# A state-space mixer beside a ternary FFN: segment sums moved into the FFN stage, steps 0 to 10 and the end put in another order

## The chip, the cores and the metric

The kernel runs on one NeuronCore of a Trainium2 chip. The core has a matrix engine (PE, with its weight loads listed as PEld), a vector engine (DVE), a scalar engine for activations and copies (ACT), a general engine (POOL) and a sync engine (SP). SP's work here is to issue DMAs; POOL issues some too. Each engine works through its own queue in order, and semaphores tie the queues together. The metric is the device time of one execution in microseconds (us); lower is better.

## The reference

The input is `x` of 4 batches of 256 tokens with 512 features. A layer norm gives `xn`; the result is `x + s * silu(f)`. `f` is a gated FFN of inner width 1792 with ternary weights, and `s` is a Mamba-2 mixer with 128 heads of 64, 8 groups and a state of 128:

```
zxbcdt = xn @ in_proj_w.T                       # gate 8192 | x 8192, B 1024, C 1024 | dt 128
xBC    = silu(conv1d(xBC, 4 taps) + conv_b)     # x, B, C
dt     = softplus(dt + dt_bias);  Adt = -exp(A_log) * dt
L      = exp(segment_sum(Adt))                  # out[i, j] = sum of Adt over m = j+1 .. i
y      = (C B^T * L) @ (x * dt) + carried state + D * x
y      = y * silu(gate); y = y * rsqrt(mean(y^2 over a group) + eps) * norm_w
s      = y @ out_proj_w.T
f      = (silu(xn @ gate_w.T) * (xn @ up_w.T)) @ down_w.T
```

The segment sum is what the change is about. It makes, for each head, a lower triangle of partial sums along 128 positions out of one row of `Adt`, and its exponential is the decay mask.

## The kernel before, in words

All of it is float32, tokens along the free dimension: `xnT` holds the normalised input transposed, 128 features by 1024 tokens, four times. The projection is cut into tiles of 128 output features. One tile of x is two heads, so there are 64 tiles (`CT`), 8 to a group (`PER_G`). A tile's gate and x features are projected together by a scheme of seven products instead of eight (`product`, L170); it needs four sums of weight blocks per tile (`combine_to`, L139 to L147, called s1, s2, s4, s3).

There are two stages. The first, `front` (L189 to L573), normalises x and runs the FFN. It has 28 FFN steps (14 tiles of the inner width, twice over half of the tokens); each has three places where `next(pieces)` (L540, L551, L564) puts in one **turn** of side work. `all_pieces` (L481) deals this side work out: dt and its rows (`dt_pieces`), then eight chains `bc_pieces`, one per group, that start every eight turns from turn 11 on, project B and C, convolve them and store the masked scores `C B^T`. A chain is 14 turns long, so two overlap. From turn 20 on `early_pieces` (L469) works beside them: it loads the weights of tiles 1 to 11, forms the four weight sums on DVE (tiles `wq` and `sq`) and stores them in the DRAM tile `early`. FFN weights come as int32 on SP's queue, two FFN steps ahead (`load_ffn`), and POOL casts them (`cast_ffn`, L225).

The second stage is the main loop (L766): 64 **steps**, one per tile, and two more that drain it. Step i projects tile i, makes the segment sums of tile i (`decay_scan`, L612), finishes tile i-1 (transposes, `values_0`, `values_1`, the mask `meet`, the products `y_products`, L655) and gates tile i-2 (`y_gate`, L668). From step 10 on it also carries the output projection of a group that is complete (`project_out`, two steps for each batch, eight steps for a group). The row of a head is loaded to all partitions (`load_rows`, L595), scanned on DVE, exponentiated on ACT (`decay_exp`) and multiplied with the scores (`gm`). `LEAD` (9) tells until which tile SiLU and the exponentials wait for the next step; `EARLY` (11) until which tile the stored weight sums are read.

The order on each engine is the program's order (`tc.manual_schedule`); what a step issues first on an engine stands first in that engine's queue. Tiles come from pools with few buffers, and a tile waits for the last reader of the one whose buffer it takes: the rows `m` have five, projection weights `w` two, PSUM banks `ps_proj` three, `ps_o` two, `ps_y` two, `ps_t` one.

After the loop the last group is projected (L950 to L990): per batch, seven products, summed on DVE into the rows fetched from `acc`, times the FFN's result, plus x.

Of the kernel before, what the change touches and what calls it, by code (L numbers as in the profile page):

```python
# [50 lines left out]
P = 128  # L51
# [23 lines left out]
LEAD = 9  # L75
# [6 lines left out]
def mixer_ffn(ctx: ExitStack, tc: tile.TileContext, x, in_w, conv_w, conv_b, dt_bias, a_log, d_col,  # L82
# [44 lines left out]
    early = dram.tile([EARLY, P, 4, KT // 2, P], F32, name="early")  # L127
# [59 lines left out]


    def front(pre, one_of, fp, f2, hp, wq):  # L189
# [279 lines left out]
        def early_pieces():  # L469
            for n in range(EARLY):  # L470
                w = wq.tile([P, 2, KT, P], F32, name="wq")
                for m, i in enumerate((n + 1, CT + n + 1)):
                    nc.sync.dma_start(w[:, m], in_w[i])
                for _ in range(2):
                    yield
                s = wq.tile([P, 4, KT // 2, P], F32, name="sq")
                yield from combine_to(s[:, 0], s[:, 1], s[:, 2], s[:, 3], w)
                nc.sync.dma_start(early[n], s)
                yield

        def all_pieces():  # L481
# [3 lines left out]
            while chains or later or turn < 11 + 8 * G:  # L485
# [4 lines left out]
                if turn == 20:  # L490
                    later.append(early_pieces())
# [42 lines left out]
        for n, (h, f) in enumerate(steps):  # L534
# [33 lines left out]
            last = pfs, f, hh, hl, wd  # L568
        down(*last)
# [3 lines left out]
        return held["a"]  # L573

    with (tc.manual_schedule(), tc.tile_pool(name="pre", bufs=NT) as pre,
          tc.tile_pool(name="one_of", bufs=1) as one_of, tc.tile_pool(name="fp", bufs=3) as fp,
          tc.tile_pool(name="f2", bufs=2) as f2, tc.tile_pool(name="hp", bufs=1) as hp,
          tc.tile_pool(name="wq", bufs=1) as wq):
        a = front(pre, one_of, fp, f2, hp, wq)
# [15 lines left out]
    def load_rows(ct):  # L595
        ms = []
        for h in range(2):
            m = mp.tile([P, T], F32, name="m")
            nc.sync.dma_start(m, rows[2 * ct + h, 0:T].partition_broadcast(P))
            ms.append(m)  # L600
        return ms
# [8 lines left out]

    def decay_scan(m):
        nc.vector.tensor_tensor_scan(m, m, after, 0.0, ALU.add, ALU.mult)  # L612
# [42 lines left out]
    def y_products(ps, vs, ms, offs):  # L655
# [4 lines left out]
        for b in range(NB):  # L660
            py = ps[b // 2][:, b % 2, :]
            for q, v, stop in ((0, v0, True), (1, v1, False), (1, v0t, True)):
                for h, d in enumerate(halves):
                    m = off[h][:, b, :] if v is v0t else diag[h][:, b, q, :]
                    nc.tensor.matmul(py[d, q * P:(q + 1) * P], v[:, b, h, :], m,  # L665
                                     start=False, stop=stop, skip_group_check=True)
# [9 lines left out]
    def come(k):  # L676

        return max(k // 2, k - 2)

    def norm_sums(sqacc):  # L680
        pv = ps_o.tile([P, NT], F32, name="pv", tag="o")
# [79 lines left out]
    with tc.manual_schedule():  # L761
# [3 lines left out]
        sqacc = rs = ya = outs = left = nxt = ob = sa = sb = sc = None  # L765
        for i in range(CT + 2):  # L766
            r, g = i % PER_G, i // PER_G
            here, old, older = i < CT, 0 <= i - 1 < CT, 0 <= i - 2 < CT
# [29 lines left out]
            if not here:  # L798
                project_out(lambda: None)
            if i + 1 <= EARLY:  # L800
                w = wp.tile([P, 2, KT, P], F32, name="w")
                nc.sync.dma_start(w[:, 0], in_w[i + 1])
                nc.sync.dma_start(w[:, 1, 0:2], early[i, :, 3])
                nc.sync.dma_start(w[:, 1, 2:4], in_w[CT + i + 1, :, 2:4])
            elif i + 1 < CT:
# [23 lines left out]
            if here:  # L829
# [5 lines left out]
                if i:  # L835
# [3 lines left out]
            if old:  # L839
# [5 lines left out]
                yps[i - 1] = y_begin(i - 1, xTs[i - 1])  # L845
            if here:
                product(px, s3, t3, False)
                product(pz, a12, x21, False, (1,))
                nc.scalar.copy(xpad_h[1], by_batch(px))
            if og >= 0 and on == 0:  # L850
                sd = norm_sums(sqacc)
            for k in range(PER_G):
                if wg >= 0 and wn == come(k) + 1:
                    wo = wos[wg][:, k, :]
                    nc.scalar.mul(wo, wo, nw[:, wg * PER_G + k:wg * PER_G + k + 1])
            if older:
                yf = yg.rearrange("p b l -> p (b l)")
                if (i - 2) % PER_G == 0:
                    sqacc = sqp.tile([P, T], F32, name="sqacc")
# [178 lines left out]
```

## Time and profile before

| | |
|---|---|
| median of three runs | 1774.26 us (1771.61 to 1774.85) |
| the profiled execution | 1773.71 us |
| its span, first to last instruction | 1771.7 us |
| FFN stage | to about 311 us; step 0's first product is at 308.60 |
| steps 2 to 8 | 17.27 us each (first product to first product) |
| step 9, step 10 | 18.40 and 28.66 us |
| steps 11 to 63 | 21.13 and 22.86 us in turn, 24.56 at a group's first |
| behind step 63 | from 1687.09 us |

The span is measured from the first to the last instruction of the program. In a timeline each line has the start in us, the length in us, the engine, the line of the kernel, the operation, the tiles (out <- in) and the count; in brackets stands how long the engine was idle before and what ended that. In the chain of waits, a line is a piece of the work that ended last: start, length, engine and line. In the windows the length is followed by the busy time and instruction count of PE, PEld, DVE, ACT and POOL, the granted clock of PE as a share of full speed, the DMA engines' busy share and GB/s.

### The profile page before, as it was taken

The page shows a single profiled execution, that of the slowest core. Times are in us where ns is not written, and L with a number is a line of the kernel's source. Part 1 is how long each engine was busy: PE and PEld are TensorE (multiplying, and loading weights), DVE is VectorE, ACT ScalarE, POOL GpSimd, SP SyncE. Part 2 cuts the span into 40 slices and gives each one's busy share as a digit, 9 for nine tenths or more (in the row PEclk, how much of TensorE's full clock was granted, in tenths as well). Part 3 has the DMA queues.
Part 4 walks back from the last instruction along what each step waited for, and adds up shares of the span by engine and source line. Part 5 has one row for each costly group of instructions (what it writes and reads, how often), then busy time and mean ns, then how long its engine had stood idle before and what let it go on. Part 6 is the DMA issues. An engine that isn't in the chain of part 4 may idle for free.

```text
span 1771.7 us, 22592 instructions
## 1 busy us (share of the span) xinstructions
PE 1733.2 (98%) x8494; PEld 1110.2 (63%) x8494; DVE 1447.3 (82%) x1740; ACT 1065.8 (60%) x1417; POOL 198.2 (11%) x239
## 2 busy tenths in 40 slices
PE   9999999999999999999999999999999999999989
PEld 6566666454466666666666666666666666666667
DVE  5757675799988898889888988898889888988956
ACT  4544333577666666666666666666666666666630
POOL 3221221000000000111011101110111011101110
PEclk9999999999999999999999999999999999999989
DMA  6254553567746675777676767776777677767684
GB/s 226 78 190 154 202 179 119 204 195 237 232 163 205 199 211 187 205 200 211 187 205 199 211 187 205 199 211 187 205 199 211 188 205 199 206 193 205 181 214 142
DMA packets 164235, 342.69 MB, mean 193 GB/s; under 512 B 15392, under 2 KB 55968, under 8 KB 164128
## 3 DMA queue, kind: packets, MB, share of 16 engines
q1 hardware_dynamic: 141296, 287.78, 47.0%
q0 software_dynamic: 22832, 53.49, 17.0%
q8 instruction: 67, 1.10, 0.3%
q14 instruction: 40, 0.33, 0.1%
HBM read 236.08 MB, written 76.28 MB: 176 GB/s over the span
## 4 chain that ended last, share of the span: by engine, by line
PE 85%; DVE 11%; ACT 2%; issue 2%; DMA 1%; ACTq 0%; DVEq 0%; SPq 0%
PE px L173 24%; PE po L721 22%; PE pq L173 13%; PE py L665 9%; PE pz L173 6%; PE pp L285 4%; PE tp L624 3%; DVE m L612 2%; PE pf L293 2%; DVE xT L181 2%; PE pg L460 1%; DVE cT L181 1%; PE pv L683 1%; DVE m L618 1%; DVE mo L619 1%
## 5 line engine op out<-in xcount | busy, mean ns | idle before, releaser
L612 DVE TENSOR_TENSOR_SCAN m<-m,after 128x1024 f32<-128x1024 f32 x128 | 291.9, 2281 | 0.0
L173 PE MATMUL px<-xc,w 128*128 128x512 f32 x576 | 279.2, 607 | 4.9 <-ACT xpad L424 2.7
L181 DVE SCALAR_TENSOR_TENSOR xT<-xpad,cw,xT 128x1024 f32<-128x1024 f32 x192 | 246.1, 1282 | 4.6
L721 PE MATMUL po<-wo,ya 128*128 128x256 f32 x768 | 178.4, 382 | 0.0
L173 PEld LDWEIGHTS px<-xc,w 128*128 128x128 f32 x576 | 99.3, 190 | 115.4 <-issue 69.4
L665 PE MATMUL py<-m,v 128*64 128x128 f32 x2048 | 161.9, 278 | 4.1 <-DVE v L641 4.1
L618 DVE TENSOR_TENSOR m<-m,gm 128x1024 f32<-128x1024 f32 x128 | 154.7, 1209 | 8.7 <-ACT m L615 8.7
L721 PEld LDWEIGHTS po<-wo,ya 128*128 128x128 f32 x768 | 142.6, 192 | 17.6 <-issue 0.3
L907 POOL DMA_DIRECT2D sqacc<-sq x55 | 46.9, 853 | 906.6 <-ACT sq L863 903.2
L173 PE MATMUL pz<-xnT,w 128*128 128x512 f32 x288 | 145.8, 592 | 0.0
L173 PE MATMUL px<-xc,s 128*128 128x512 f32 x288 | 137.5, 600 | 5.0 <-ACT pz L822 2.2
L173 PE MATMUL px<-xnT,w 128*128 128x512 f32 x288 | 142.0, 615 | 0.2 <-DMA w<-in_in_w 0.2
L173 PE MATMUL pq<-xnT,s 128*128 128x512 f32 x288 | 136.2, 595 | 3.3 <-DVE xpad L872 3.3
L615 ACT ACTIVATE m<-m 128x1024 f32<-128x1024 f32 x128 | 135.4, 1058 | 0.7
L173 PE MATMUL pq<-xc,s 128*128 128x512 f32 x288 | 135.4, 592 | 0.0
L665 PEld LDWEIGHTS py<-m,v 128*64 128x64 f32 x2048 | 117.8, 137 | 26.2 <-issue 19.6
L721 PE MATMUL po<-tw,sy 128*128 128x256 f32 x512 | 116.8, 381 | 0.8 <-ACT sa L775 0.8
L624 PEld LDWEIGHTS tp<-ident,xT 128*128 128x128 f32 x512 | 63.8, 141 | 71.9 <-issue 57.6
L721 PEld LDWEIGHTS po<-tw,sy 128*128 128x128 f32 x512 | 97.9, 191 | 14.7 <-ACT sa L775 1.2
L672 DVE TENSOR_TENSOR yg<-py,gT 128x512 f32<-128x512 f32 x128 | 83.8, 677 | 22.4 <-PE py L665 22.4
L832 ACT COPY gT<-px 128x512 f32<-128x512 f32 x64 | 37.4, 584 | 105.1 <-PE px L173 105.1
L173 PEld LDWEIGHTS px<-xc,s 128*128 128x128 f32 x288 | 54.7, 192 | 73.1 <-issue 65.8
(172 smaller groups left out, 3065.1 us busy)
## 6 DMA issues: line engine op xcount, KB each, us to landing
m<-rows SPq DMA_DIRECT2D x128, 512.0 KB, 6.5
w<-in_in_w SPq DMA_DIRECT2D x133, 256.0 KB, 6.8
mo<-rows SPq DMA_DIRECT2D x128, 256.0 KB, 7.2
gated<-yg SPq DMA_DIRECT2D x64, 512.0 KB, 8.2
ya<-gated SPq DMA_DIRECT2D x30, 1024.0 KB, 7.1
sqacc<-sq POOLq DMA_DIRECT2D x55, 512.0 KB, 5.7
wo<-in_out_w SPq DMA_DIRECT2D x64, 256.0 KB, 7.2
acc<-sa POOLq DMA_DIRECT2D x24, 512.0 KB, 6.0
```

The source lines that it names most:

```text
L173: nc.tensor.matmul(pp, a[:, k, :], b[:, k, :], start=start and k == 0, stop=k == KT // 2 - 1, skip_group_check=not start)
L181: nc.vector.scalar_tensor_tensor(xT, xpad[:, :, k:k + L], cw[:, i, k:k + 1], xT, ALU.mult, ALU.add)
L285: nc.tensor.matmul(pp, w[:, k * P:(k + 1) * P], part[:, k, :], start=(k == 0 and part is xh), stop=(k == KT - 1 and part is xl))
L612: nc.vector.tensor_tensor_scan(m, m, after, 0.0, ALU.add, ALU.mult)
L615: nc.scalar.activation(m, m, AF.Exp)
L618: nc.vector.tensor_mul(m, m, gm[:, 0:T])
L624: nc.tensor.transpose(tp[:, b, :], xT[:, b, c * P:(c + 1) * P], ident)
L665: nc.tensor.matmul(py[d, q * P:(q + 1) * P], v[:, b, h, :], m, start=False, stop=stop, skip_group_check=True)
L672: nc.vector.tensor_mul(yg[:, 2 * i:2 * i + 2, :], ps[i], by_batch(gT[:, i * HALF:(i + 1) * HALF]))
L721: nc.tensor.matmul(po, a[:, k, :], b[:, k, :], start=start and k == 0, stop=k == HG - 1, skip_group_check=not start)
L832: nc.scalar.copy(gT[:, HALF:], px)
L907: nc.gpsimd.dma_start(sqacc, sq, accum_op=ALU.add)
```

## The change

It has four parts.

1. **Segment sums beside the FFN.** `early` no longer holds weight sums but finished segment sums: 22 rows (two heads for each of tiles 0 to 10). `early_pieces` loads a row to all partitions (three buffers in the pool `ep`, where `wq` had one of each of two tiles), scans it in turns 2, 3 and 5 of every eight, counted from a chain's start, and stores 512 KB. The first two loads are issued in turn 18. The weight sums of the first tiles go back to the steps.
2. **Steps 0 to 10.** The main loop loads the scanned rows of these tiles and doesn't scan. In steps 0 to 9 (`fill`) the square of the gated tile goes ahead of the copy of xpad's second half, `y_begin` behind it; the weight sums for the next tile come in two halves, around the taps; the first tap goes ahead of `values_1`; and `y_products` takes the products that need v1 last. `LEAD` is 10.
3. **Tile 1's weights** are loaded at the end of the FFN, so step 0 loads none.
4. **The end.** The two draining steps are written out by hand. Tile 63's transpose goes ahead of group 6's last output products, which are dealt around it; `sa` and `sb` take buffers of `w` and `s`; the last tile is gated and squared in halves; the norm sums take the `ps_t` bank; the output weights of the last group are loaded two per step, in its first four steps.

```diff
-LEAD = 9
+LEAD = 10
...
-    early = dram.tile([EARLY, P, 4, KT // 2, P], F32, name="early")
+    early = dram.tile([2 * EARLY, P, T], F32, name="early")
...
-        def early_pieces():
-            for n in range(EARLY):
-                w = wq.tile([P, 2, KT, P], F32, name="wq")
-                for m, i in enumerate((n + 1, CT + n + 1)):
-                    nc.sync.dma_start(w[:, m], in_w[i])
-                for _ in range(2):
-                    yield
-                s = wq.tile([P, 4, KT // 2, P], F32, name="sq")
-                yield from combine_to(s[:, 0], s[:, 1], s[:, 2], s[:, 3], w)
-                nc.sync.dma_start(early[n], s)
+        def early_pieces(phases=(2, 3, 5)):
+            ms, n, turn = {}, 0, 18 - 11
+            while n < 2 * EARLY:
+                if turn % 8 in phases and turn > 9:
+                    m = ms.pop(n)
+                    decay_scan(m)
+                    nc.sync.dma_start(early[n], m)
+                    n += 1
+                for k in range(n, min(n + 2, 2 * EARLY)):
+                    if k not in ms and (turn % 8 not in phases or k == n):
+                        ms[k] = ep.tile([P, T], F32, name="em")
+                        nc.sync.dma_start(ms[k], rows[k, 0:T].partition_broadcast(P))
+                turn += 1
                 yield
...
-                if turn == 20:
+                if turn == 18:
                     later.append(early_pieces())
...
+        w = load_w(1, CT + 1)
         down(*last)
         ffn_out(1, pfs)
...
-            nc.sync.dma_start(m, rows[2 * ct + h, 0:T].partition_broadcast(P))
+            n = 2 * ct + h
+            nc.sync.dma_start(m, early[n] if ct < EARLY else rows[n, 0:T].partition_broadcast(P))
...
-    def y_products(ps, vs, ms, offs):
+    def y_products(ps, vs, ms, offs, last_v1):
...
+        parts = [(0, v0), (1, v1), (1, v0t)]
+        order = [(b, *p) for b in range(NB) for p in parts]
+        if last_v1:
+            order = [(b, *parts[n]) for ns in ((0, 2), (1,)) for b in range(NB) for n in ns]
...
-    def come(k):
-        return max(k // 2, k - 2)
+    def come(g, k):
+        return k // 2 if g == G - 1 else max(k // 2, k - 2)
...
-        for i in range(CT + 2):
+        for i in range(CT):
...
-            if i + 1 <= EARLY:
-                w = wp.tile([P, 2, KT, P], F32, name="w")
-                nc.sync.dma_start(w[:, 0], in_w[i + 1])
-                nc.sync.dma_start(w[:, 1, 0:2], early[i, :, 3])
-                nc.sync.dma_start(w[:, 1, 2:4], in_w[CT + i + 1, :, 2:4])
-            elif i + 1 < CT:
+            fill = og < 0
+            if 0 < i < CT - 1:
                 w = load_w(i + 1, CT + i + 1)
...
-                if i:
+                if i >= EARLY:
                     decay_scan(ms[i][0])
...
-                yps[i - 1] = y_begin(i - 1, xTs[i - 1])
+                if not fill:
+                    yps[i - 1] = y_begin(i - 1, xTs[i - 1])
...
+            if older and fill:
+                square()
             if here:
                 product(px, s3, t3, False)
                 product(pz, a12, x21, False, (1,))
                 nc.scalar.copy(xpad_h[1], by_batch(px))
+            if old and fill:
+                yps[i - 1] = y_begin(i - 1, xTs[i - 1])
...
-                if i == 0:
-                    decay_scan(ms[i][0])
-                    decay_scan(ms[i][1])
                 product(pq, s4, x22, False)
-            if old and og < 0:
-                vs.append(values_1(i - 1, xTs[i - 1]))
+            if fill:
+                s = scp.tile([P, 3, KT // 2, P], F32, name="s")
+                sums = combine_to(s[:, 0], s[:, 1], s[:, 2], blocks(w)[2], w)
+                a = factors(w, s)
+                next(sums)
+                xTs[i] = xtp.tile([P, NB, L], F32, name="xT")
+                last_tap(i, xTs[i], xpad)
+                conv_taps(i, xTs[i], xpad, (0,))
+                if old:
+                    vs.append(values_1(i - 1, xTs[i - 1]))
...
-                conv_taps(i, xTs[i], xpad)
+                conv_taps(i, xTs[i], xpad, (1, 2) if fill else (0, 1, 2))
...
-                if i + 1 <= EARLY:
-                    s = scp.tile([P, 3, KT // 2, P], F32, name="s")
-                    nc.sync.dma_start(s, early[i, :, 0:3])
-                    a = factors(w, s)
+                if fill:
+                    next(sums)
...
-                if i:
+                if i >= EARLY:
                     decay_scan(ms[i][1])
...
-        whole = {0: fetch(0), 1: fetch(1)}
-        yas[2] = load_gated(G - 1, 2)
+        last, ob = CT - 1, NB - 1
+        yg = y_gate(yps.pop(last - 1), gTs.pop(last - 1))
+        nc.sync.dma_start(gated[last - 1], yg.rearrange("p b l -> p (b l)"))
+        yas = {b: load_gated(G - 1, b, PER_G - 1) for b in range(2)}
+        decay_exp(ms[last][1])
+        py = y_begin(last, xTs[last])
+        vs = values_0(last, transposed(xTs[last], 0))
+        for m, off in zip(ms[last], offs[last]):
+            meet(m, off)
+        sa = wp.tile([P, NC, KT, P], F32, name="w").rearrange("p n k m -> p n (k m)")
+        sb = scp.tile([P, 3, KT // 2, P], F32, name="s")[:, 0:2].rearrange("p n k m -> p n (k m)")
+        sc = osp.tile([P, HH], F32, name="sc", bufs=2)
+        outs = out_first(left, rights[G - 2], leave)
+        for _ in range(2):
+            next(outs)
+        vs.append(values_1(last, xTs[last]))
+        sq = sqp.tile([P, T], F32, name="sq")
+        nc.scalar.activation(sq, yg.rearrange("p b l -> p (b l)"), AF.Square)
+        nc.vector.tensor_add(sqacc, sqacc, sq)
+        for _ in range(2):
+            next(outs)
+        y_products(py, vs, ms.pop(last), offs.pop(last), False)
+        rights[G - 1], toms = right_factors(wos[G - 1])
+        for make in toms[0:2]:
+            make()
+        whole = {0: fetch(0)}
+        yg, gT = ygp.tile([P, NB, L], F32, name="yg"), gTs.pop(last)
+        sq = sqp.tile([P, T], F32, name="sq")
+        for n in range(2):
+            two, to = slice(2 * n, 2 * n + 2), slice(n * HALF, (n + 1) * HALF)
+            nc.vector.tensor_mul(yg[:, two, :], py[n], by_batch(gT[:, to]))
+            nc.scalar.activation(sq[:, to], yg[:, two, :].rearrange("p b l -> p (b l)"), AF.Square)
+        nc.sync.dma_start(gated[last], yg.rearrange("p b l -> p (b l)"))
+        for n in range(2):
+            to = slice(n * HALF, (n + 1) * HALF)
+            nc.vector.tensor_add(sqacc[:, to], sqacc[:, to], sq[:, to])
         for b in range(2):
             nc.vector.tensor_copy(yas[b][:, PER_G - 1, :], yg[:, b, :])
-        sd = norm_sums(sqacc)
         left, sums = left_factors(yas[0])
-        rights[G - 1], toms = right_factors(wos[G - 1])
-        for make in (sums[0], toms[0], sums[1], toms[1], *sums[2:], *toms[2:]):
+        for make in (sums[0], sums[1], toms[2], sums[2], sums[3]):
             make()
+        for _ in outs:
+            pass
+        toms[3]()
+        rows_b = batch_rows(acc, ob)
+        nc.gpsimd.dma_start(rows_b, sa, accum_op=ALU.add)
+        nc.gpsimd.dma_start(rows_b[:, 0, :], sb.rearrange("p n c -> p (n c)"), accum_op=ALU.add)
+        nc.gpsimd.dma_start(rows_b[:, 1, HH:], sc, accum_op=ALU.add)
+        whole[1] = fetch(1)
+        yas[2] = load_gated(G - 1, 2)
+        sd = norm_sums(sqacc, ps_t, "t")
```

## The prediction

> **What bounds the kernel now.** I read the page's busy shares first, then the chain of waits by windows, then windows cut at the starts of the steps (a step is one pass of the main loop; its first product, px from xnT, marks the start), then the timelines of single engines.
>
> ```profile
> PE 1733.2 (98%) x8494; PEld 1110.2 (63%) x8494; DVE 1447.3 (82%) x1740; ACT 1065.8 (60%) x1417; POOL 198.2 (11%) x239
> ...
> L612 DVE TENSOR_TENSOR_SCAN m<-m,after 128x1024 f32<-128x1024 f32 x128 | 291.9, 2281 | 0.0
> ```
> ```profile
> 361.43:378.70 17.27, 16.59 (x87) 8.57 (x85) 15.88 (x17) 13.43 (x17) 0.89 (x1) 1.00 0.73 236
> 465.04:483.44 18.40, 16.59 (x87) 8.56 (x85) 18.15 (x19) 12.32 (x15) 0.85 (x1) 1.00 0.85 263
> 483.44:512.10 28.66, 26.45 (x134) 17.05 (x132) 24.34 (x26) 18.03 (x23) 0.00 (x0) 0.94 0.39 131
> 512.10:533.23 21.13, 21.13 (x110) 13.10 (x108) 17.50 (x20) 14.93 (x21) 0.84 (x1) 1.00 0.70 225
> ...
> 665.19:689.75 24.56, 24.56 (x135) 16.49 (x133) 22.41 (x28) 15.83 (x22) 1.76 (x2) 1.00 0.48 145
> ```
> The first two lines are the page's engines and the costliest group. The windows are steps 3, 9, 10, 11 and 18, with the busy time of PE, PEld, DVE, ACT and POOL, the granted clock and the DMA share behind the length. From step 11 to step 63 PE never stops. Steps 2 to 10 are another matter: DVE has 15.9 of 17.27 us and PE pauses. The chain there runs through the scans (first lines), and PE's own timeline shows what it waits for:
>
> ```profile
> 345.98 2.20 DVE m L612
> 348.19 1.18 DVE yg L672 x2
> 349.37 2.20 DVE m L612
> ```
> ```profile
> 355.67 1.98 PE L173 MATMUL pq<-xnT,s 128*128 128x512 f32 x4 [0.26 <-DVE xpad L872]
> ...
> 358.88 0.44 PE L665 MATMUL py<-m,v 128*64 128x128 f32 x4 [0.41 <-DVE v L641]
> ...
> 489.35 3.61 PE L173 MATMUL px<-xc,s 128*128 128x512 f32 x4 [2.21 <-ACT pz L822]
> ```
> The end is the other place where PE stands (PE's timeline, behind step 63's last product at 1687.09; at 1691.64 it had waited 0.83 for ACT's write to sa):
>
> ```profile
> 1700.19 0.63 PE L624 MATMUL tp<-ident,xT 128*128 128x128 f32 x4 [4.40 <-DVE v L632]
> ...
> 1713.72 2.76 PE L683 MATMUL pv<-one,sqacc 128*128 128x1 f32 x16 [2.77 <-DVE sqacc L909]
> 1716.34 3.76 PE L721 MATMUL po<-wo,ya 128*128 128x256 f32 x8
> ```
> Its chain names the cause of the 4.40: an accumulating DMA of 5.6 us and one of 4.2 that ACT's writes to sa and sb wait for, with an exponential and everything behind it queued on ACT.
>
> **What a step costs PE alone.** Step 11 takes 21.13 and holds 24 instructions of output product at 5.18 in the chain: 15.95 without. Step 18 is 24.56 with 6.91 of output product and 1.70 of norm sums: 15.95 again. That is the floor of a step without output products (0 to 9).
>
> **Steps 2 to 8.** Each loses two scans (2.20 each in the chain) and gains four weight sums (0.42 each): DVE falls from 15.9 to 13.2 us. I place the rest from the ACT and DVE rows of the step at 344.16, times from the step's start. ACT is as before up to the copy to gT (6.0 to 6.5), which PE's third product waits for, so that stays at 6.6. The multiplications by the mask follow the exponentials (6.1 to 9.7); xpad's sum ends at 10.4, before PE wants it (11.1), so the 0.26 goes. Values 0 end at 11.6, the weight sums at 12.4. The first tap waits for ACT's last tap (ends 13.1) and ends at 14.4; v1 follows to 15.05. PE reaches the y products at 13.4, and in the new order 32 of 48 need no v1 (1.85 us), so v1 is wanted at 15.2: the 0.41 goes with 0.15 to spare. Two more taps, then sums, end at 18.8, that is 2.8 into the next step, where DVE waits for an exponential until 6.1 anyway; SiLU starts at 2.6 as now. So a step is 16.05, with 0.1 of pipeline restarts: 7 x 1.22 = 8.5. In steps 3 and 4 ACT has two output-weight scalings ahead of the copy that v1's chain waits for: minus 0.5. **8.0.** SP's list shrinks (two weight loads instead of three and one of sums; the scanned rows are as large as the raw ones), so DMA at 0.73 is no worse.
>
> **Step 9** still has the two right-factor sums (1.22 each) ahead of xpad's sum and ahead of v1: 0.45 of waiting before pq and 0.9 before v1's products, about 17.5 against 18.40: **0.9**. **Step 10** waits 2.21 for a copy behind a late SiLU, and the granted clock is 0.5 for 3.41 us behind that pause (1.7 lost). With step 9's taps ending 2.0 into step 10, SiLU, exponential and copy are on time: 24.75 (step 18's 24.56 and 0.2 for xpad's sum behind the left sums). **3.9.**
>
> **Steps 0 and 1.** Step 0 has two scans in the chain (3.19), but removing them moves the first tap only from 324.45 to about 322.7, where last_tap becomes what it waits for (the ffn store that held it till 321.93 lands sooner, as SP no longer issues 0.9 MB of weights and sums around it). Taps, SiLU, table load, exponential and copy follow, so PE's product at 332.45 starts 1.35 earlier; v1's 0.41 goes too: **1.8.** The pause before it was 2.18 with a granted clock of 0.5 for 3.41 us behind it; now about 1.7, and pauses of 1.62 and 1.68 in the FFN had none. I keep the half clock; losing it too is 1.7, kept as the range's lower end. The Trainium skill ("TensorE: Matmul & The Clock Gate", section on why this matters) asks for a pause of about 3 us before the clock drops; the rows at 332.45 and 489.35 dropped at 2.2, so the measurement decides. By the page alone the shorter pause would keep the full clock, and the sum below would be 27.7 instead of 26.0.
>
> **The end.** From 1687.09 to 1716.34 PE takes 29.25, and the final 4 x 12.09 of output product take 50.96 instead of 48.36 because the clock is halved behind the pauses. The new order puts every product behind something done in time. T0 (xT's SiLU ended at 1685.9), two output products, T1 (values 0 done by 1689.1), two more products while meet and v1 finish (1693.2), y products, the last three, norm sums (squares added by 1700.1, wanted at 1703.0). sa and sb lie in free buffers, so the DMA wait goes. All output weights are loaded and scaled by step 62. That is 7 x 1.727 + 2 x 0.43 + 2.77 + 1.70 = 17.4: gain 29.25 - 17.4 + 2.6 = 14.4. Where it may slip: DVE stands on the copy into yas[1] till its load lands (1701.6 now), and the reciprocal comes behind the last factor sum at about 1706.7, 1.3 before PE needs the bank. I take 0.7 off: **13.7**; lower end 8 if these loads land 5 us late, for fetch(0) and SP's stores share that queue.
>
> **The FFN stage pays.** 22 scans of 2.28 are 50.2; the 44 sums that leave are 21.9 (groups sq at L142 to L146). DVE has 143.8 busy in 85.7 to 308.3, 78.8 free, so 28.3 more fits in total. They fall into turns 2, 3 and 5 of the eight that a bc chain's start is apart, where the rows show pauses of 1.8 to 3.8 us on DVE (at 211.85, 222.47, 242.62); I followed the three ways in which eight turns lie against the FFN's steps of three turns and found delays of 0.5 to 1 us in the taps behind turn 5, while the sums that go had caused PE pauses of 0.94 (140.76) and 1.06 (232.57). Net +1.0 - 2.0. One place is worse: the first two row loads are issued behind the store of adt and ahead of a weight load that is in the chain.
>
> ```profile
> 75.94 0.89 SPq L133 DMA_DIRECT2D w<-in_in_w  x2
> ```
> ```profile
> 76.40 5.20 DMA w<-in_in_w
> ```
> ```profile
> 77.46 3.71 POOL L225 CAST wg<-wg_i 128x512 fp32r<-128x512 int32 x1 [6.99 <-DMA wg_i<-in_gate_t]
> ```
> The three lines are SP's timeline, the chain, and POOL's timeline. The chain goes on from w through the weight sums, a tap and ACT's copy to PE's product at 84.74. SP would stand till the store of adt (issued at 73.74) lands at 76.72, and 1 MB goes ahead of w: 2.6 us at the pace of two row loads (325.71, 327.03), 3.7 at that of the loads here. I take 3.3; ends 0 and 5.2 (the row again). Sum of the stage: **+2.3**, ends -3 and +9. Each scan is followed by a store that SP waits for, and a load three scans later waits for that store to land; behind them stand the FFN's weights, loaded two FFN steps ahead, so a few us are free. "SBUF — State Buffer", on who interferes with whom, says that a Vector instruction with two SBUF inputs shuts out a GpSimd one for its whole length. The cast of 3.71 us (median 0.616) around the scan at 78.48 (L350, 2.28) agrees, and by that rule the 50.2 us of scans close POOL. POOL is busy 42.7 of those 222.6 us and its casts run an FFN step ahead, so I leave them uncounted.
>
> **Sum:** 2.3 - 1.8 - 8.0 - 0.9 - 3.9 - 13.7 = -26.0, against the profiled execution's 1773.71 (span 1771.7), which is 0.55 under the median 1774.26. So 1748.
>
> **Rivals.** (1) The scans land on the FFN's path, and it is slower: at 2.28 each it costs 50.2 against 28.3 saved, 1796; it decides from 1.3 us per scan. For it: DVE is in order and holds hl and the bank releases. Against: 78.8 us free. 0.04. (2) Casts or weights are late about once per three scans, 1 us each, 7 more: 1755. For it: the stretched cast, SP's stores. 0.17. (3) v1's 0.15 is missed, or ACT is what holds steps 2 to 8 and the order does not shorten them as said: 0.6 a step is 1752.5, no shortening 1756. Against: ACT has 13.4 of 17.27. 0.11. (4) The end keeps a pause on ya or the reciprocal and a half clock: 1754. 0.09. (5) FFN pays nothing and step 1 keeps its clock: 1743. 0.09. The forecast, 1745 to 1751: 0.50.
>
> **Numbers.** The range 1742 to 1758 takes in (2) to (5) and leaves out (1) and pairs of mishaps. A change under 0.2% (3.5 us) cannot be told from none here; faster 0.93, same 0.02, slower 0.05.
>
> **What would show it.** Right: no m scan in steps 0 to 10, steps 2 to 8 at 16.0 to 16.2, step 10 near 24.8 at full clock, under 20 us from step 63's end to the first final product, step 0 starting 1 to 4 us later. Wrong: PE pauses before L285 or L293 after each group of scans, or a wait on v at 0.4 still there.

## The result and the profile after

The changed kernel takes 1757.42 us (median of four, 1757.17 to 1759.62) against 1772.93 for the kernel before (1771.23 to 1774.85): ratio 0.9915, 95% interval 0.9898 to 0.9932. The forecast was 1748, with a range to 1758. The profiled execution took 1759.62 us (span 1757.9), 14.1 less than the one of before, where the sum said 26.0. It is the slowest of the four (the others took 1757.17 to 1757.53), and the medians differ by 15.5, so some 1.4 us of what the traces below show as lost belongs to these two executions and not to the kernels.

Page of the kernel after, engines and the costliest group. DVE's busy time hardly changes: 22 of its scans are no longer named m but em.

```profile
PE 1730.6 (98%) x8494; PEld 1112.3 (63%) x8494; DVE 1444.6 (82%) x1742; ACT 1067.0 (61%) x1418; POOL 203.6 (12%) x238
...
L189 DVE TENSOR_TENSOR_SCAN m<-m,after 128x1024 f32<-128x1024 f32 x106 | 241.9, 2282 | 0.0
```

Windows of the kernel after, steps 1, 3, 5, 9, 10 and 11 (columns as before: length, PE, PEld, DVE, ACT, POOL, granted clock, DMA share, GB/s). PE no longer stops in steps 2 to 8, and steps 1 and 10 have full clock.

```profile
338.30:356.71 18.41, 16.38 (x85) 8.48 (x84) 14.16 (x19) 12.82 (x17) 0.00 (x0) 1.00 0.23 88
...
372.81:389.13 16.32, 16.32 (x86) 8.65 (x85) 12.90 (x19) 13.47 (x18) 0.89 (x1) 1.00 0.77 226
405.45:421.56 16.11, 16.11 (x87) 8.67 (x85) 13.01 (x19) 13.08 (x17) 0.84 (x1) 1.00 0.69 213
469.86:487.27 17.41, 16.59 (x86) 8.56 (x84) 15.08 (x21) 12.34 (x16) 0.85 (x1) 1.00 0.82 247
487.27:512.29 25.02, 24.99 (x135) 16.43 (x133) 20.19 (x29) 18.01 (x24) 0.00 (x0) 1.00 0.34 115
512.29:533.41 21.12, 21.12 (x110) 13.09 (x108) 17.50 (x20) 14.92 (x21) 0.84 (x1) 1.00 0.68 225
```

PE's timeline behind step 63 (first line its last group of four): transposes, output products, y products, norm sums and the first final product follow one another without a wait.

```profile
1686.87 0.39 PE L674 MATMUL py<-mo,v 128*64 128x128 f32 x4
1687.19 0.66 PE L630 MATMUL tp<-ident,xT 128*128 128x128 f32 x4
...
1697.58 0.39 PE L674 MATMUL py<-mo,v 128*64 128x128 f32 x4
...
1703.18 1.84 PE L692 MATMUL pv<-one,sqacc 128*128 128x1 f32 x16
1704.89 1.32 PE L730 MATMUL po<-wo,ya 128*128 128x256 f32 x5
```

So the account from one trace to the other, by the starts of the steps' first products:

| part | forecast | measured |
|---|---|---|
| FFN stage (step 0 starts at 324.46, before 308.60) | +2.3 | **+15.9** |
| steps 0 and 1 | -1.8 | -3.3 |
| steps 2 to 8 (16.10 each, 16.32 in 3 and 4) | -8.0 | -7.7 |
| step 9, step 10 | -0.9, -3.9 | -1.0, -3.7 |
| steps 11 to 62 | 0 | -0.1 |
| from step 63's start | -13.7 | -14.1 |

The first line is far off; steps 0 and 1 won 1.5 more than said, and the rest came as said. In the FFN's lines below, `xh` and `xl` are the two parts into which an operand is split (`hh` and `hl` likewise), `pf` is the PSUM bank of the down projection, `xt` (with `ds_bc`) empties it, and the change of halves is where the FFN goes on to its second half of the tokens. In the FFN stage two B/C chains take much longer. Windows from the start of one chain to that of the next, first the kernel before, then after:

```profile
71.14:105.78 34.64, 32.42 (x131) 21.38 (x130) 24.35 (x30) 15.43 (x20) 10.31 (x10) 1.00 0.61 207
166.72:198.32 31.60, 29.98 (x117) 19.78 (x116) 22.89 (x34) 12.22 (x18) 6.32 (x9) 1.00 0.55 193
```
```profile
71.83:111.58 39.75, 34.10 (x131) 22.23 (x130) 28.58 (x29) 15.59 (x20) 10.69 (x9) 0.96 0.60 201
171.86:211.78 39.92, 33.72 (x118) 22.12 (x117) 26.04 (x30) 12.51 (x18) 6.66 (x9) 0.91 0.63 214
```

They are 5.1 and 8.3 us longer, with a granted clock below 1. In the first one (timelines of SP, DVE and PE, after) the weights `w` of the next chain are issued behind two row loads, at 78.39 instead of 75.94; DVE stands 4.25 us for them, and PE 4.52:

```profile
77.48 0.81 SPq L484 DMA_DIRECT2D em<-rows  x2
78.39 1.33 SPq L133 DMA_DIRECT2D w<-in_in_w  x2
```
```profile
85.71 0.42 DVE L142 TENSOR_TENSOR s<-w 128x256 f32<-128x256 f32 x1 [4.25 <-DMA w<-in_in_w]
```
```profile
88.89 3.29 PE L173 MATMUL px<-xc,w 128*128 128x512 f32 x4 [4.52 <-ACT xpad L427]
```

In the second one SP came to the store of a segment sum and stood there until the scan was done. That scan is late itself, behind the four sums xl of the change of halves. Scores, a row and FFN weights follow in SP's list, and only then the chain's weights, 3.6 us behind the chain's start. In before they were issued 3.1 ahead of it (SP):

```profile
163.66 1.00 SPq L133 DMA_DIRECT2D w<-in_in_w  x2
```

DVE, SP and PE of the kernel after:

```profile
164.37 3.32 DVE L282 TENSOR_TENSOR xl<-xnT,xh 128x512 fp32r<-128x512 f32 x4 [1.56 <-ACT xh L281]
...
168.87 2.38 DVE L189 TENSOR_TENSOR_SCAN em<-em,after 128x1024 f32<-128x1024 f32 x1
...
182.30 0.43 DVE L142 TENSOR_TENSOR s<-w 128x256 f32<-128x256 f32 x1 [3.70 <-DMA w<-in_in_w]
```
```profile
171.28 0.33 SPq L479 DMA_DIRECT2D early<-em  x1
171.66 0.42 SPq L470 DMA_DIRECT2D scores<-sc  x1
172.14 0.77 SPq L484 DMA_DIRECT2D em<-rows  x1
173.01 1.14 SPq L220 DMA_DIRECT2D wg_i<-in_gate_t  x1
...
175.41 0.92 SPq L133 DMA_DIRECT2D w<-in_in_w  x2
```
```profile
187.36 2.78 PE L173 MATMUL px<-xc,w 128*128 128x512 f32 x4 [3.64 <-ACT xpad L427]
...
195.41 0.80 PE L296 MATMUL pf<-wd,hh 128*128 128x512 f32 x1 [2.13 <-DVE xt L304]
```

A third place, a pause of 2.19 in front of a product with hl at 307.15, has a scan and four taps ahead of hl on DVE. Behind the pauses of 4.52, 3.64, 2.13 and 2.19 the granted clock is 0.5 for 3.41 us each time; before had no such stretch in the FFN stage. Four of them at half speed lose 6.8 us if PE is busy throughout, so by this estimate some two fifths of the 15.9 are clock, not waiting.

### The profile page after: what moved, and what is told of

It reads as the page before. It is cut to its first block, busy times and chain, and to the rows that moved or that the text cites. A ratio compares the mean times of both kernels' runs of the same rounds, so it can differ in the third digit from the quotient of the medians.

```text
span 1757.9 us, 22580 instructions
## 1 busy us (share of the span) xinstructions
PE 1730.6 (98%) x8494; PEld 1112.3 (63%) x8494; DVE 1444.6 (82%) x1742; ACT 1067.0 (61%) x1418; POOL 203.6 (12%) x238
## 4 chain that ended last, share of the span: by engine, by line
PE 89%; DVE 4%; DMA 4%; ACT 1%; issue 1%; SPq 1%; POOL 0%; ACTq 0%; POOLq 0%; DVEq 0%
PE px L173 27%; PE po L730 22%; PE pq L173 13%; PE py L674 10%; PE pz L173 7%; PE tp L630 3%; PE pp L288 3%; DMA w<-in_in_w 2%; PE pf L296 2%; PE pg L463 1%; PE pv L692 1%; DVE em L189 1%; DVE cT L181 1%; DVE bT L181 1%; DMA ffn<-xt 0%
## 5 line engine op out<-in xcount | busy, mean ns | idle before, releaser
L173 PE MATMUL px<-xc,w 128*128 128x512 f32 x576 | 280.1, 609 | 11.4 <-ACT xpad L427 9.8
L189 DVE TENSOR_TENSOR_SCAN m<-m,after 128x1024 f32<-128x1024 f32 x106 | 241.9, 2282 | 0.0
L674 PE MATMUL py<-mo,v 128*64 128x128 f32 x1024 | 99.4, 273 | 0.0
L884 DVE TENSOR_TENSOR xpad<-xpad,pq 128x512 f32<-128x512 f32 x64 | 43.7, 683 | 67.3 <-ACT xpad L865 67.3
```

The lines of the kernel that those rows point to most:

```text
L173: nc.tensor.matmul(pp, a[:, k, :], b[:, k, :], start=start and k == 0, stop=k == KT // 2 - 1, skip_group_check=not start)
L884: nc.vector.tensor_add(xpad_h[1], xpad_h[1], by_batch(pq))
```

## The experiments

The theories: **1**, SP's order makes the chains' weights late, with a half clock behind each pause; **2**, the scans' own time on DVE does it; **3**, the DMA engines are short of bandwidth. "Step 0" below is the start of step 0's first product in the profiled execution. Where theories spoke of 1757, that is the changed kernel.

### SP's order, in two sizes

**w_first**: the row loads start one turn later, behind the weights of turn 19.

```diff
-            ms, n, turn = {}, 0, 18 - 11
+            ms, n, turn = {}, 0, 19 - 11
...
-                if turn == 18:
+                if turn == 19:
```

> The first two row loads are issued in turn 19, behind the weights that this turn loads, and so everything of the segment sums starts one turn later; nothing else is changed. Theory 1 (SP's queue: the 15.9 us that the FFN stage lost are weights of the next chain that land late because row loads and stores of segment sums stand ahead of them on SP, plus a stretch of half clock behind each PE pause): the pause of 4.52 us in front of the px product at 88.89 falls to about the 1.08 of before and the half clock at 89.42 (1.7 us lost) goes, 5.1 us less; step 0's first product at about 319.4, time about 1752.3, ratio to the kernel before about 0.9886. Theory 2 (the scans' own 50.7 us on DVE delay the FFN's sums): the same scans stand on DVE, so the stage still takes 324 and the time stays at 1757, ratio 0.9915. Theory 3 (the DMA engines are too busy with 23 MB more of rows and stores): the same bytes move, no change either.

Measured: 1754.13 (1751.95 to 1755.31), ratio 0.9883 (0.9866 to 0.9899); step 0 at 319.49. The pause is 1.03, its half clock is gone, the chain takes 34.61 instead of 39.75. In that trace this is the whole 5 us. The medians differ by 3.3, less than the 5.1 expected; the next place of loss still had its pause (3.93).

**w_early**: a chain's weights three turns earlier.

```diff
+        def load_bc(g):
+            return load_w(2 * CT + G + g, 2 * CT + g) if g < G else load_w(0, CT)
...
-            w = load_w(2 * CT + G + g + 1, 2 * CT + g + 1) if g + 1 < G else load_w(0, CT)
+            w = held.pop("w2") if g else load_bc(1)
...
             product(pq, s4, x22, False)
+            if g + 2 <= G:
+                held["w2"] = load_bc(g + 2)
```

> The weights for the next chain are issued in turn 5 of a chain instead of turn 0 of the following one, three turns earlier, ahead of that turn's segment sum and its store; the row loads and scans stand as in the changed kernel. As this also puts the weights of turn 19 ahead of the first row loads, theory 1 (SP's queue and the half clock) expects both places to close: 5.1 us at 88.89 and some 8 of the 8.3 us that the turns from 171.86 to 211.78 lost; step 0's first product at about 311, time 1744, ratio 0.984. Theory 2 (DVE's own time in the scans): no change, 1757, ratio 0.9915. Theory 3 (DMA bandwidth): weights issued earlier still share the engines, so the two places shrink by less than half, 1751 to 1757.

Measured: 1746.02 (1744.31 to 1748.36), ratio 0.9842 (0.9828 to 0.9857); step 0 at 309.65, 14.8 of the 15.9 back (the medians differ by 11.4). Theory 1 holds for most of it, with the same scans and the same bytes, so theories 2 and 3 fall as its main cause. The weight sums no longer wait (DVE's timeline of this run, which also shows what is left: a scan directly ahead of the product that frees a bank):

```profile
172.11 0.42 DVE L142 TENSOR_TENSOR s<-w 128x256 f32<-128x256 f32 x1
...
181.45 2.45 DVE L189 TENSOR_TENSOR_SCAN em<-em,after 128x1024 f32<-128x1024 f32 x1
183.82 0.66 DVE L304 TENSOR_TENSOR xt<-pf,ds_bc 128x512 f32<-128x512 f32 x1
```
```profile
184.54 0.51 PE L296 MATMUL pf<-wd,hh 128*128 128x512 f32 x1 [2.35 <-DVE xt L304]
```

One stretch of half clock is left in this FFN stage, from 293.26 on behind a pause of 2.05 at 292.39. The pause of 2.35 has none, though expectations further down put one behind it too.

**w_early_late**: besides, the store of a segment sum is issued in the turn behind its scan.

```diff
+                if done:
+                    nc.sync.dma_start(early[n - 1], done)
+                    done = None
...
-                    m = ms.pop(n)
-                    decay_scan(m)
-                    nc.sync.dma_start(early[n], m)
+                    done = ms.pop(n)
+                    decay_scan(done)
```

> As the run with the weights three turns earlier, and each store of a segment sum is issued one turn behind its scan, so that SP never stands at it while the scan runs. Theory 1: if SP's standing at the stores is what holds the FFN's weights too, another 1 to 3 us go, 1741 to 1743; if the weights of the chains were all of it, the same as the run without the later stores, 1744. Theory 2: still 1757.

Measured: 1746.04 (1745.17 to 1746.74), ratio 0.9841 (0.9827 to 0.9856), step 0 at 310.75: no difference. With the chains' weights out of its way, SP's standing at the stores costs nothing that shows; the FFN's own weights have lead enough.

### The scans by themselves

**no_scan** leaves the scans out (`decay_scan(m)` in `early_pieces` deleted), **w_early_no_scan** does that with the weights three turns earlier.

> Leaves out the 22 scans in the FFN stage; rows are loaded and stored as they are, so the segment sums of tiles 0 to 10 are missing from the computation and the masks of these tiles are wrong. Order, loads and stores are the changed kernel's. Theory 1 (SP's queue): the late weights at 88.89 stay, with their half clock (5 us), for no scan stands there yet; at 182 SP no longer stands at a store behind a scan, so most of the 8.3 go; step 0's first product at 313 to 317, time 1746 to 1750, ratio 0.985 to 0.987. Theory 2 (DVE's time in the scans): all 15.9 go and some of what the weight sums took, step 0 at 305 to 309, time 1738 to 1742, ratio 0.980 to 0.982.

> The weights three turns earlier, and the 22 scans left out (rows are loaded and stored raw, so the segment sums of tiles 0 to 10 are missing from the computation). Beside the run with the scans (309.65) it measures what the scans alone cost in DVE's queue once SP's order is mended. Theory 1b: the pauses of 2.35 and 2.05 and their half clocks, so step 0 at about 302, time 1738, ratio 0.980. Rival (the loads and stores of the 22 rows are what costs, through SP and the DMA engines): no change against the run with the scans, 309 and 1745. Rival 2 (each of the 22 scans costs part of its 2.3 us): step 0 below 298.

Measured: 1744.37 (1742.99 to 1745.30), ratio 0.9831 (0.9817 to 0.9846), and 1738.90 (1738.21 to 1739.69), ratio 0.9806 (0.9790 to 0.9822). With the two runs above they make a square (step 0, median):

| | with the scans | without |
|---|---|---|
| weights at the chain's start | 324.46, 1757.4 | 307.19, 1744.4 |
| weights three turns earlier | 309.65, 1746.0 | 303.75, 1738.9 |

In the traces late weights alone cost 3.4 us, the scans alone 5.9, both together 20.7; in the medians 5.5, 7.1 and 18.5. The first run's time falls between its two theories. Its pause at the first place stays (3.42), as theory 1 had it, but without a scan SP has nothing to stand at (there the weights are issued at 166.04, 2.5 ahead of the chain's start), the second place vanishes whole, and step 0 starts where theory 2 had it. So beside what each costs by itself there is a part that takes both, the scan that holds SP while the weights wait in SP's list: 11.4 us in these traces, 5.9 in the medians. How large it is stays open between the two, as each trace has its own half clocks. Of the second run's theories, 1b came in (step 0 a little later than its 302); loads and stores cost nothing that shows.

### Where the scans stand

**w_early_turns** (three scans from turns 45, 46 and 72 to 78, 79, 80) and **w_early_turns2** (to 43, 47 and 75), both on w_early; `early_pieces` gets a list of turns.

```diff
-                if turn % 8 in phases and turn > 9:
+                if turn in at:
...
+            at = [t for t in range(21, 78) if (t - 11) % 8 in (2, 3, 5) and t not in (45, 46, 72)]
+            at += [78, 79, 80]               # w_early_turns
+            at = sorted(at + [43, 47, 75])   # w_early_turns2
```

> As the run with the weights three turns earlier (step 0's first product at 309.65, 1746.0), and the segment sums of turns 45, 46 and 72 are made in turns 78, 79 and 80 instead, all others in the turns they had. Theory 1b (what is left of the scans' cost is three scans that stand in DVE's queue directly ahead of sums the FFN waits for: two ahead of the products with ds_bc at the change of halves, where PE waits 2.35 us, one ahead of four taps and hl, where it waits 2.05): both pauses go, and the half clock behind each (1.7) with them; step 0 at about 302, time about 1738, ratio to the kernel before 0.980. Rival (any 22 scans cost the same somewhere: the last turns have no free place either): the pauses come back between 300 and 310, step 0 stays at 309 to 311, time 1745 to 1747, ratio 0.984.

> The weights three turns earlier, and the segment sums of turns 45, 46 and 72 are made in turns 43, 47 and 75 instead (not in four turns in a row at the end, where DVE stood 3.83 and 4.98 us for a row that was still on its way, because three buffers do not cover four scans in a row). Theory 1b (position in DVE's queue): the pause of 2.35 at the change of halves goes as it went with the turns at the end (198 instead of 199.4 at the chain that starts there), and the one near 290 falls from 2.05 to the 1.7 or 1.9 that stand there with no scan in turn 72 at all; no row is waited for; step 0's first product at 304 to 306, time 1740 to 1742, ratio 0.982. Rival (22 scans have to cost somewhere): pauses of about 2 us in front of the products with hl of turns 43 to 48 or 75, step 0 at 308 to 310, time 1745, ratio 0.984.

Measured: 1751.40 (1750.64 to 1752.54), ratio 0.9877 (0.9862 to 0.9892), and 1748.31 (1747.91 to 1749.40), ratio 0.9859 (0.9842 to 0.9875). Both missed, and both are slower than w_early. In the first, four scans in a row outran three buffers, and hl stood behind a scan that waited for its row (DVE, then PE):

```profile
311.03 2.29 DVE L189 TENSOR_TENSOR_SCAN em<-em,after 128x1024 f32<-128x1024 f32 x1 [4.98 <-DMA em<-rows]
313.24 0.67 DVE L579 TENSOR_TENSOR hl<-sg,hh 128x512 fp32r<-128x512 f32 x1
```
```profile
313.96 0.79 PE L296 MATMUL pf<-wd,hl 128*128 128x512 f32 x1 [7.16 <-DVE hl L579]
```

In the second, the scan of turn 43 stands ahead of the weight sums that the chain starting there needs, and that of turn 75 ahead of a tap of bT, whose SiLU a product of the scores waits for (2.70). The first place, DVE and PE:

```profile
172.26 2.29 DVE L189 TENSOR_TENSOR_SCAN em<-em,after 128x1024 f32<-128x1024 f32 x1
174.46 0.77 DVE L142 TENSOR_TENSOR s<-w 128x256 f32<-128x256 f32 x1
```
```profile
180.51 2.55 PE L173 MATMUL px<-xc,w 128*128 128x512 f32 x3 [3.06 <-ACT xpad L430]
```

The wait for the bank at the change of halves did go in both, as theory 1b (position in DVE's queue) said. So position decides, and I had chosen worse ones.

**w_early_47** moves turn 46's scan to turn 47, and **w_early_47_80** that of turn 72 to turn 80 as well (the list shown is the second run's).

```diff
+            at = [t for t in range(21, 78) if (t - 11) % 8 in (2, 3, 5) and t not in (46, 72)]
+            at = sorted(at + [47, 80])
```

> The weights three turns earlier (1746.0, step 0's first product at 309.65), and one segment sum moved: the one of turn 46 is made in turn 47. In the run with the weights earlier, the scan of turn 46 stood from 181.45 to 183.82 ahead of the last product with ds_bc, which frees the bank that the next product with hh waits for (2.35, and a half clock behind it). The 22 scans together cost 5.9 us there (309.65 against 303.75 without them), 4.0 of them in the chain from 165.64 to 199.37. Theory 1b (position): these 4 us go, for turn 47's place has only the products of the C tile behind it; step 0 at about 306, time 1742, ratio 0.982. Rival (the scan of turn 47 only moves the wait to hl or to the sums behind pz, as the three other placings did): step 0 at 309 to 312, time 1745 to 1748, ratio 0.984 to 0.986.

> As the run with turn 46's segment sum in turn 47, and the one of turn 72 in turn 80, three turns behind the one of turn 77, so that its row has landed. Theory 1b: the pause of 2.05 near 290 falls to the 1.72 that stands there without any scan, its half clock goes, and nothing new comes, for DVE has idle time behind 295; 1 to 2 us less than the run with turn 47 alone, step 0 at 304 to 305, time 1740 to 1741, ratio 0.981. Rival (the last store stands ahead of tile 1's weights on SP, or the scan ahead of hl): step 0 or step 1 is later by what was won, the same as with turn 47 alone or up to 4 us above.

Measured: 1742.82 (1742.10 to 1742.98), ratio 0.9829 (0.9811 to 0.9846), step 0 at 307.05, and 1740.70 (1740.60 to 1741.48), ratio 0.9819 (0.9802 to 0.9837), step 0 at 305.00. The second came as theory 1b had it. The first came near: step 0 won 2.6 us of the 4 it was to win, with a half clock behind the pause of 2.17 that was left at 289.77. The last is the fastest kernel of this study with the full computation: 16.7 us below the changed kernel, and 1.25 us of step 0's start from the run without scans. What PE still waits for between 60 us and its step 0 (sums of waits: us, times, longest), first the kernel after up to 324.46:

```profile
PE px L173 <- ACT xpad L427: 9.8, 5, 4.5
PE pf L296 <- DVE hl L572: 3.8, 3, 2.2
PE pf L296 <- DVE xt L304: 2.1, 1, 2.1
```
```profile
PE pf L296 <- DVE hl L579: 2.8, 2, 1.7
PE px L173 <- ACT xpad L430: 1.9, 2, 1.0
PE pg L468 <- ACT bT L186: 0.5, 1, 0.5
```

### The steps and the end

**old_order**: `fill = False` in the steps (not in every place the order of before, as shown below). **v1_as_before**: only `y_products` gets `False` for `last_v1`.

> The changed kernel with steps 0 to 9 in the order of before (square behind the copy of xpad's half, y_begin ahead of it, the weight sums after the taps, values 1 ahead of the first tap, the products with v1 where they were); the segment sums stay in the FFN stage, LEAD stays 10. Theory (from the prediction: leaving out the scans and the new order each remove part; the order removes 0.41 before the products with v1 and 0.26 before pq): steps 2 to 8 at 16.5 to 16.8 instead of 16.1, time 1761 to 1764, ratio 0.994. Rival A (the scans alone were it): 16.1, 1757, ratio 0.9915. Rival B (the chain through v1 and the taps holds the step whatever DVE's load, so the order is nearly all of it): 17.0 or more, 1766 and above, ratio 0.996.

> The changed kernel, with the products of y in the order of before (those with v1 second of three for each batch), everything else in the new order. Theory (the new product order is what makes room for the first tap ahead of values 1): in steps 2 to 8 values 1 end 1.9 us behind the first product of y and are wanted 0.3 us behind it, so PE stands about 1.6 us in each, 17.5 to 17.8 a step instead of 16.1, time 1768 to 1772, ratio 0.997 to 0.999. Rival (the order of the products is worth the 0.41 wait of before alone): 16.5 a step, 1760 to 1761, ratio 0.993.

Measured: old_order 1767.22 (1765.62 to 1770.98), ratio 0.9969 (0.9956 to 0.9982), steps 2 to 8 at 16.85; v1_as_before 1773.57 (1771.86 to 1777.46), ratio 1.0005 (0.9995 to 1.0014), steps 2 to 8 at 17.58 (17.86 in 3 and 4). PE waits for v1 in both, first old_order, then v1_as_before:

```profile
405.85 0.44 PE L674 MATMUL py<-m,v 128*64 128x128 f32 x4 [0.57 <-DVE v L647]
```
```profile
411.61 0.44 PE L674 MATMUL py<-m,v 128*64 128x128 f32 x4 [1.53 <-DVE v L647]
```

In one place old_order is not the order of before: on DVE the sum into gT stands ahead of v1, and behind it in before (before, then old_order):

```profile
358.13 0.69 DVE L641 TENSOR_TENSOR v<-tp,dt 128x512 f32<-128x512 f32 x1 [1.31 <-PE tp L624]
358.74 0.68 DVE L888 TENSOR_TENSOR gT<-gT,pq 128x512 f32<-128x512 f32 x1
```
```profile
404.50 0.69 DVE L905 TENSOR_TENSOR gT<-gT,pq 128x512 f32<-128x512 f32 x1 [1.54 <-PE pq L173]
405.11 0.68 DVE L647 TENSOR_TENSOR v<-tp,dt 128x512 f32<-128x512 f32 x1
```

PE's wait for v1 is 0.57 there and 0.41 in before, so an estimated 0.16 us a step of old_order is this place. Measured, taking two scans out of a step and the four weight sums in (DVE from 15.9 to 13.1 us) brings 0.42 us and the new order the other 0.75; by the estimate the very order of before would give 0.58 and 0.59, which no run tested. With the tap ahead of values 1 but the products as they were the step is slower than before the change. So DVE's load alone did not bound these steps; v1's place in the order did as much. By the step the first theory of each run came nearest (old_order a little above its 16.5 to 16.8, by less than the 0.16). Both times lie above what that theory said. In old_order steps 0 and 1 took 34.34 us instead of 32.25, with PE waiting 3.59 for a weight sum at 342.83, and by its time alone rival B would be nearest.

**end_only**: the kernel before with the written-out end alone (the part of the diff from `last, ob = CT - 1, NB - 1` on, with `come`, `norm_sums` and the loop's length).

> The kernel before with the fourth part of the change alone: the end in its own order, the output weights of the last group two per step, sa and sb in free buffers. Theory (the parts are independent): the 13.9 us that the two profiles show behind step 63 come in full, 1759.5, ratio 0.992. Rival (part of it comes from the rest, through SP's shorter lists or the phase of the clock's windows): 3 to 6 us less gain, 1763 to 1766, ratio 0.994 to 0.996.

Measured: 1758.54 (1757.97 to 1758.92), ratio 0.9917 (0.9902 to 0.9931). From step 63's start to PE's last product it takes 87.42, the same as in the changed kernel (before 101.50). The end is worth its 14 us alone. So the changed kernel is the end's gain and about 1 us (1758.54 against 1757.42) for all the rest together: the steps won 15.7 us, and the FFN stage took 15.9.

## Why the prediction was right, and where it wasn't

The time lies in the range, at its upper end; faster was right. That it lies inside is in part luck: one stage lost 13.6 us more than said, 0.6 us more would have carried the median out, and the profiled execution, 1759.62, is out. By the prediction's own steps:

- **The FFN stage pays** is the step that failed: +2.3 with an upper end of 9, measured +15.9; its own sign of being right, step 0 1 to 4 us later, did not come. Its term for the first late weights was sound as a size (3.3, ends 0 and 5.2; w_first gives 5.1 for the pause and its half clock of about 1.7) but left out the half clock. The second place was not seen at all. The prediction asked what stands behind SP's wait at a store and named only the FFN's weights, which have two FFN steps of lead (w_early_late: no effect, right). It passed over the chains' weights in the same list, which are issued when a chain starts and are wanted 6.5 us later (in w_early 172.11, the chain's start being 165.64). The square of four runs shows that a large part of the loss takes both, the scan that holds SP and the weights behind it.
- The net of +1.0 and -2.0 for scans against weight sums: with SP's order mended, the scans cost 5.9, and the stage without them starts step 0 4.85 earlier than before (this includes weights that come sooner than before, so it isn't the sums alone). The balance measured with SP's order mended is +1.05 (309.65 against 308.60), where -1.0 was said. It is 2 us off, and each term was too small, and "pauses of DVE" was too coarse a measure: it matters which sum stands next behind the scan.
- Casts uncounted: right. With the weights early POOL is busy 88.7 us up to step 0 with the scans and 75.7 without, so there the scans do stretch the casts, as the Trainium skill says ("SBUF — State Buffer", who interferes with whom), but PE's list of waits holds none on them. In the changed kernel itself they do not add up to anything: 76.4 with the scans, 77.3 in no_scan. Of its 84 casts 6 overlap a scan, of w_early's 17.
- **Steps 2 to 8** right in size and mechanism: v1 ends 15.25 into step 4 and PE's products with it start at 15.30. **Steps 9 and 10** right.
- **Steps 0 and 1**: 1.5 better than said. The pause at step 1 fell to 1.54, and the half clock, kept in the sum, went. The term that was mis-sized is that clock, which the text had as the range's lower end. Part of this is the draw of before's profile: end_only has before's steps and the same pause, without the half clock, and its step 1 takes 19.58 instead of 21.31.
- **The end** right: 17.70 from step 63's end to the first final product (17.4 said), and the final batches at full clock.
- Of the rivals, the second (weights late, 1755) is the nearest in time and half in kind: weights, not casts; two places of 5 and 8 us, not 1 us at every third scan. The fifth, by its own terms (2.3 and 1.7), is 1744 and not 1743.

## What to carry to other kernels

Before a store that waits for a long instruction is put into a DMA queue, list everything issued behind it and ask of each load when it is wanted; the load with no lead decides, and issuing it before the store cost nothing that shows here. When work is dealt into an in-order engine's idle time, what counts is not the idle sum but which instruction stands next behind each piece, and who waits for it; five placings of the same 22 scans gave 1740.7 to 1751.4. Taking load off the busiest side engine may bring no more than a new order of what stays on it (0.42 against 0.75 us a step here, or an estimated 0.58 against 0.59).

## What the hardware showed unexpectedly

The half clock follows a fixed grid of 3.41 us within an execution, and the grid lies differently in each. What counts is how much of a pause falls into one grid window, not how long it is. The same pause of 2.18 us in front of step 1's product px is in the kernel before and in end_only. Windows on each grid, first before, then end_only:

```profile
328.83:332.24 3.41, 0.98 (x5) 0.42 (x4) 2.02 (x2) 3.38 (x4) 0.00 (x0) 1.00 0.33 134
332.24:335.65 3.41, 3.20 (x4) 1.51 (x5) 3.28 (x4) 2.31 (x4) 0.00 (x0) 0.50 0.00 0
```
```profile
328.40:331.81 3.41, 2.11 (x8) 0.80 (x6) 2.76 (x2) 2.79 (x3) 0.00 (x0) 1.00 0.64 249
331.81:335.22 3.41, 2.19 (x5) 1.06 (x6) 2.68 (x3) 3.41 (x6) 0.00 (x0) 1.00 0.01 4
335.22:338.63 3.41, 3.41 (x9) 1.44 (x8) 2.69 (x5) 1.30 (x3) 0.00 (x0) 1.00 0.00 0
```

In before, 1.97 us of it fall into one window (PE busy 0.98), and the next window has half clock. In end_only it is cut into 0.95 and 1.24, and the clock stays. Step 1 takes 21.31 us in the first and 19.58 in the second, 1.7 less. Over the 14 profiled executions, for pauses over 1.4 us: all 25 windows with 1.90 us or more of pause were followed by half clock, none of those with 1.77 or less, and two of the eight between. A pause of 3.59 us in old_order, cut into 1.80 and 1.79, had none. The Trainium skill ("TensorE: Matmul & The Clock Gate", part 1) has the free-running window of this length, and the runs agree; it asks for an idle window, and here a window idle for 1.90 of 3.41 us was enough. So a pause of 2 us costs 0 or about 1.7 us more by chance, and two single profiles can differ by that without a cause in the kernel.
